# Two transposes moved behind the fourth attention product, with residuals ahead of normalizations and the fifth weight block behind the first left half

## The chip, the cores and the metric

The kernel runs on one core of one Trainium2 chip. The metric is the device time of one execution in microseconds; before the change it is 353.28 us, the median of three runs (352.8 to 354.54).

## What is computed

The reference is one transformer-like layer on 2048 rows of 1024 numbers, with post-normalization. Cut to what matters:

```python
attn = jnp.einsum('ds,td->st', w1, w2) * sparse_mask        # 1024 x 1024, a band
x = layernorm(x + gelu(x @ attn + b2))                      # "attention"
w_l = dequant_kbit(qweight, lut4, 4)                        # 4-bit codes, 16 entries for each row
w_h = dequant_kbit(qweight, lut8, 8)
y = where(norm(x) > 64, x @ w_h.T, x @ w_l.T) + bias        # "ffn"
out = layernorm(x + y)
```

With these inputs no row has a norm over 64, so the kernel computes the 4-bit path alone, counts the rows (and the mask's entries outside the band) that would need more, and runs a general path behind a branch that is not taken here.

## The kernel before

**Tiles.** The 2048 rows are 16 row tiles x0 to x15 of 128 x 1024 in float32. The weight of the second product is dequantized in eight blocks of 128 output rows (numbered 0 to 7), each transposed into its 128 columns of `wT`. The identity matrix is added to the diagonal of each block (L349), so that the product contains the residual already.

**The first stage** forms `attn` on TensorE (PE) in eight band products (L464), each masked on VectorE (DVE, L486). Between them runs the dequantization of the first blocks.

**A block of the weight** is made by a generator, `dequantize_pair` (L309), which yields after each half of a block; `steps(n)` issues n halves. One half consists of three ScalarE (ACT) activations (L329, tiles `e`), one GpSimd (POOL) instruction (L333, tile `root`) and three predicated copies on DVE (L336, L337, L338). A second half ends with one more copy that selects between the two roots (L346) and the small addition of the identity (L349). `transpose_pending(left)` (L358) transposes finished blocks into `wT`: for each block eight PE transposes (L281) into two PSUM tiles `pt` and two ACT copies out of them (L282). There are four `pt` buffers in all.

**The list `todo`** (L831) gives the order of the second stage: attention 0 to 3; then left 0, attention 4, left 1, attention 5, left 2, attention 6, left 3, attention 7; then attention 8 to 11; then right 0, attention 12, and so on. The second product of row tiles 4 to 15 is done in pairs by `ffn_pair`, which the change does not touch.

- **attention n** (L577): ten PE products onto a PSUM tile `mm` that already holds `b2` (L556; `mm` has two buffers, and ACT fills them in L505, `fill_b2`); Gelu on ACT into `z` (L581; two buffers); the residual x + z on DVE with a row sum (L585); then `stats` (L383): the mean on POOL (`nm`, L387), the sum of squares on ACT (`junk`, L390), the reciprocal root on POOL (`r`, L392 and L393). The normalization on DVE (L397) and two small POOL instructions (L591, L592) are put off into a list `later`, which `now()` empties.
- **left n and right n** (`ffn_half`, L637): eight PE products of 512 columns (L599) into `mm`, and the addition of the bias on DVE (L611, `combine`). A left half reads `wT`'s blocks 0 to 3, a right half blocks 4 to 7.
- **prepare** (L858) transposes the next entry's input. For left n it transposes the normalized row tile with its columns in another order (`early{n}`); for attention n the raw one. It does so ahead of the current entry, except for left 0: `soon` is false there, and the transposes come behind attention 3.

**What sets the order.** A scheduler orders each engine's instructions by the order in the program, dependencies and estimated times, and moves them where it sees room; from attention 8 on DVE is in program order (`manual_schedule`, L871). `tc.issue_after(ins)` adds an edge that keeps the block's instructions on `ins`'s engine behind `ins`; it costs no wait. Each engine then runs its own queue strictly in order, and waits on semaphores for the others. What matters here is therefore which instruction stands ahead of which in a queue.

The lines around the change: L868 empties `pending` (blocks 2 and 3 of the weight) at attention 3, that is before its products; L582 and L889 empty `later`; L837 lists after which entries one more half block is issued:

```python
unpack_after = [("attention", n) for n in range(3)]
unpack_after += [("left", 0), ("attention", 4), ("left", 1)]
unpack_after += [("attention", 5), ("left", 2), ("attention", 6), ("left", 3)]
```

The first two of these ten halves finish block 3; blocks 4 to 7 are the other eight.

Of the kernel before, what the change touches and what calls it, by code (L numbers as in the profile page):

```python
# [32 lines left out]
EARLY = 4  # L33
# [3 lines left out]
def window(s):  # L37

    return max(0, s * P - BAND), min(D, (s + 1) * P + BAND)
# [153 lines left out]
def kernel(  # L193
# [13 lines left out]
    nc = tc.nc  # L207
# [7 lines left out]
    with ExitStack() as main:  # L215
# [60 lines left out]
        def transpose_blocks(dst, block):  # L276

            for g in range(NH):
                pt = ps_tr.tile([P, HALF // P, P], FP, tag="tr", name="pt")
                for j in range(HALF // P):  # L280
                    nc.tensor.transpose(pt[:, j, :], block(g * (HALF // P) + j), ident)  # L281
                done = nc.scalar.copy(dst[:, g * (HALF // P) : (g + 1) * (HALF // P), :], pt)  # L282
            return done

        def transpose_columns(dst, src):
            return transpose_blocks(dst, lambda k: src[:, ts(k, P)])
# [71 lines left out]
        def transpose_pending(left):  # L358

            while len(pending) > left:  # L360
                ot, w_nat = pending.pop(0)
                transpose_columns(wT[:, :, ts(ot, P)], w_nat)
# [15 lines left out]
        def steps(n):  # L378
            for _ in range(n):
                next(low, None)  # L380


        def stats(u, total):  # L383


            nm = work.tile([P, 1], FP, tag="nm", name="nm", bufs=4)
            nc.gpsimd.tensor_scalar(nm, total, -1.0 / D, None, ALU.mult)  # L387
            junk = work.tile([P, D], BF, tag="junk", name="junk", bufs=1)
            ss = work.tile([P, 1], FP, tag="ss", name="ss", bufs=4)
            nc.scalar.activation(junk, u, AF.Square, scale=float(-D), bias=total, accum_out=ss)  # L390
            r = work.tile([P, 1], FP, tag="r", name="r", bufs=4)
            nc.gpsimd.tensor_scalar(r, ss, 1.0 / D**3, EPS, ALU.mult, ALU.add)  # L392
            nc.gpsimd.tensor_tensor(r, r, minus_half, ALU.pow)  # L393
            return nm, r, ss

        def normalize(dst, u, nm, r):
            nc.vector.tensor_scalar(dst, u, nm, r, ALU.add, ALU.mult)  # L397
# [3 lines left out]
        def load_x(pool, n):  # L401
            t = pool.tile([P, D], FP, tag=f"x{n}", name=f"x{n}")
            nc.sync.dma_start(out=t, in_=x[ts(n, P), :])
            x_tiles.append(t)
# [7 lines left out]
        with tc.tile_pool(name="prod", bufs=1) as prod:  # L412
# [47 lines left out]
            for s in range(KT):  # L460
                lo, hi = window(s)
                ps = ps_mm.tile([P, D], FP, tag="mm", name="mm")
                for k in range(KT):
                    part = nc.tensor.matmul(  # L464
                        out=ps[:, : hi - lo],
                        lhsT=w1_sb[s][:, k, :],
                        rhs=w2T[:, k, lo:hi],
                        start=(k == 0),
                        stop=(k == KT - 1),
                    )  # L470
# [3 lines left out]
                if s >= KT - 2:  # L474
# [11 lines left out]
                masked = nc.vector.tensor_tensor(  # L486
                    attn[:, s, : hi - lo], ps[:, : hi - lo], masks[s][:, : hi - lo], ALU.mult
                )
                if s >= KT - 2 - AHEAD and len(first_xT) < AHEAD:

                    n = len(first_xT)
                    xT = work.tile([P, D], FP, tag="z", name="xT", bufs=2)
# [10 lines left out]
        def fill_b2():  # L503
            ps = ps_mm.tile([P, D], FP, tag="mm", name="mm")
            nc.scalar.copy(ps, b2_bc)  # L505
            with_b2.append(ps)
# [6 lines left out]
            load_x(late, n)  # L513
        nc.sync.dma_start(out=bias_bc, in_=bias.partition_broadcast(P))

        def transposed(n, tag, bufs, by_bit):
            xT = late.tile([P, KT, P], FP, tag=tag, name="xT", bufs=bufs)
            if by_bit:
                cols = x_tiles[n].rearrange("t (b s) -> t s b", s=8)
                transpose_blocks(xT, lambda k: cols[:, k, :])  # L520
            else:
                transpose_columns(xT, x_tiles[n])
            return xT
# [17 lines left out]
        def check_outside(s):  # L541

            for raw, _, _, _, i in outside_band(s):
                nc.scalar.activation(raw, raw, AF.Abs, accum_out=outside[:, i : i + 1])

        def band_rows(xT):

            if not with_b2:
                fill_b2()
            ps = with_b2.pop(0)  # L550
            for s in range(KT):
                lo, hi = window(s)
                for h in range(NH):
                    a, b = max(lo, h * HALF), min(hi, (h + 1) * HALF)
                    if a < b:
                        nc.tensor.matmul(  # L556
                            out=ps[:, a:b],
                            lhsT=xT[:, s, :],
                            rhs=attn[:, s, a - lo : b - lo],
                            start=False,  # L560
                            stop=hi == D or (h == 0 and window(s + 1)[0] >= HALF),
                            skip_group_check=True,
                        )
            return ps
# [5 lines left out]
        def now():  # L570
            while later:
                later.pop(0)()
# [4 lines left out]
        def attention(n, xT, meanwhile=nothing):  # L577
            xt = x_tiles[n]
            ps = band_rows(xT)
            z = work.tile([P, D], FP, tag="z", name="z", bufs=2)  # L580
            nc.scalar.activation(z, ps, AF.Gelu)  # L581
            now()  # L582
            meanwhile()
            total = work.tile([P, 1], FP, tag="total", name="total", bufs=4)
            nc.vector.scalar_tensor_tensor(xt, z, 1.0, xt, ALU.mult, ALU.add, accum_out=total)  # L585
            nm, r, ss = stats(xt, total)

            def rest():
                normalize(xt, xt, nm, r)

                nc.gpsimd.tensor_tensor(ssq[:, n : n + 1], r, r, ALU.mult)  # L591
                nc.gpsimd.tensor_tensor(ssq[:, n : n + 1], ssq[:, n : n + 1], ss, ALU.mult)  # L592

            later.append(rest)
# [42 lines left out]
        def ffn_half(n, xT, h):  # L637
            ps = ps_mm.tile([P, D], FP, tag="mm", name="mm")
            product(ps[:, :HALF], xT, h)
            now()  # L640
            combine(n, h, ps[:, :HALF], bias_bc[:, ts(h, HALF)])
            if h == 1:
                finish_rows(n)
# [187 lines left out]
        todo = [("attention", n) for n in range(4)]  # L831
# [2 lines left out]
        todo += [("attention", n) for n in range(4 + EARLY, SOON)]  # L834
        for m in range(EARLY):
            todo += [("right", m), ("attention", SOON + m)]
        unpack_after = [("attention", n) for n in range(3)]  # L837
        unpack_after += [("left", 0), ("attention", 4), ("left", 1)]
        unpack_after += [("attention", 5), ("left", 2), ("attention", 6), ("left", 3)]

        kept = {}
        rows, blocks = {}, {}
# [15 lines left out]
        def prepare(what, n):  # L858
            if what == "attention":
                return first_xT[n] if n < AHEAD else transposed(n, "xT", 2, False)  # L860
            if what == "left":
                kept[n] = transposed(n, f"early{n}", 1, True)
            return kept[n]

        ready = prepare(*todo[0])
        ordered = main.enter_context(ExitStack())
        for i, (what, n) in enumerate(todo):
            if (what, n) == ("attention", EARLY - 1):  # L868
                transpose_pending(0)
            if (what, n) == ("attention", 2 * EARLY):  # L870
                ordered.enter_context(tc.manual_schedule(engines={mybir.EngineType.DVE}))  # L871
            if (what, n) == ("attention", SOON - 2):
                steps(100)
                transpose_pending(0)
                first_sb.close()
                last = main.enter_context(tc.tile_pool(name="last", bufs=1, side="right"))
                for m in range(SOON, NT):
                    load_x(last, m)
            xT = ready

            soon = i + 1 < len(todo) and todo[i + 1] != ("left", 0)
            if soon:
                ready = prepare(*todo[i + 1])
            if what == "attention":
                if n >= SOON + 1:
                    attention(n, xT, lambda: prepare_pair(EARLY, n - SOON - 1))
                else:
                    attention(n, xT)
                if n < 2 * EARLY:  # L889
                    now()  # L890
            else:
                ffn_half(n, xT, 0 if what == "left" else 1)
                if what == "right":
                    weight_sum(last, n + 1)
                    now()
            if i + 1 < len(todo) and not soon:
                ready = prepare(*todo[i + 1])
            if (what, n) in unpack_after:
                with tc.issue_after(masked.ins):
                    steps(1)  # L900
        first_ps.close()
        ps_pair = main.enter_context(
# [54 lines left out]
```

## Time and profile before

| | before |
|---|---|
| median of 3 runs | 353.28 us |
| the profiled execution | 353.46 us |
| its span in the profile | 351.7 us |
| PE busy | 325.6 us (93%) |
| DVE busy | 210.3 us (60%) |
| ACT busy | 179.1 us (51%) |
| POOL busy | 116.1 us (33%) |
| mean granted TensorE clock | 0.99 |

The span is what the profile covers; 1.8 us of the execution lie around it. A row of the profile's timeline gives a start, a duration, the engine, the line, the output and inputs, a count, and in brackets the idle time before it with what ended it. Rows of PE products overlap a little, since matmuls are pipelined; two passes are counted for each float32 product, so an attention product has twenty. The duration of DVE and ACT rows contains their write-out, and the next instruction can start about 0.1 us before the end of a row. "PEclk" is the share of the full TensorE clock that was granted.

### The profile page before, as it was taken

Reading aid. Unit: us, or ns where it says so; the run is one execution under the profiler, and the core shown is the slowest. Engines: PE = TensorE matmul, PEld = TensorE weight load, DVE = VectorE, ACT = ScalarE, POOL = GpSimd, SP = SyncE. Lnnn points to the kernel's source line nnn. Section 1 sums busy time; section 2 is a strip of 40 time slices with the busy share of each in tenths; the row PEclk is TensorE's granted clock in tenths of the full one; section 3 lists DMA queues with packets and bytes.
Section 4 is the critical chain, followed back from the end, with each engine's and each line's share of the span. In section 5 each row is a group of like instructions: output and inputs, shape, how many; then the busy total and the mean of one; then the engine's idle time right before and its main releaser. Section 6 shows DMA issues by size and latency. Waiting matters only on the chain.

```text
span 351.7 us, 3697 instructions
## 1 busy us (share of the span) xinstructions
PE 325.6 (93%) x1227; PEld 201.7 (57%) x1228; DVE 210.3 (60%) x310; ACT 179.1 (51%) x257; POOL 116.1 (33%) x162
## 2 busy tenths in 40 slices
PE   6699979759999999999999989999999998999990
PEld 6587769655775679856665534444444444444460
DVE  0659898878999853435667763544535615632342
ACT  4796987879989959856435401214115024033020
POOL 1812432793264443234352711403104005014010
PEclk9999999989999999999999999999999999999997
DMA  8999209400000000603056334253553441431103
GB/s 253 320 316 383 109 25 376 197 2 0 0 3 0 0 2 0 239 3 108 37 188 210 118 110 129 91 209 108 211 171 123 185 160 59 177 123 60 60 16 116
DMA packets 28475, 43.91 MB, mean 125 GB/s; under 512 B 7584, under 2 KB 20640, under 8 KB 28448
## 3 DMA queue, kind: packets, MB, share of 16 engines
q1 hardware_dynamic: 26832, 42.66, 35.3%
q10 hardware_dynamic: 1616, 0.93, 0.9%
q8 instruction: 12, 0.20, 0.2%
q14 instruction: 15, 0.12, 0.1%
HBM read 28.90 MB, written 14.68 MB: 124 GB/s over the span
## 4 chain that ended last, share of the span: by engine, by line
PE 72%; DVE 10%; DMA 7%; POOL 5%; issue 3%; ACT 1%; SPq 0%; POOLq 0%; DVEq 0%
PE u L716 21%; PE mm L599 16%; PE mm L556 13%; PE w L716 10%; PE v L716 6%; PE pt L281 6%; DMA w_raw<-in_L_attn_w_dram 2%; DMA w_sb<-in_L_attn_w_dram 2%; DVE e L336 2%; POOL root L333 2%; DMA x<-in_L_attn_x_dram 2%; PE mm L464 1%; DVE squares L666 1%; DVE root L346 1%; DVE root L338 1%
## 5 line engine op out<-in xcount | busy, mean ns | idle before, releaser
L390 ACT ACTIVATE junk<-x,total 128x1024 bf16<-128x1024 f32 x31 | 35.6, 1150 | 60.8 <-DVE total L624 26.8
L556 PE MATMUL mm<-attn,xT 128*128 128x198 f32 (+2 forms) x320 | 61.2, 347 | 1.1 <-ACT mm L505 1.1
L329 ACT ACTIVATE e<-v,lt,diff 128x1024 f32<-128x1024 uint8 x48 | 56.9, 1244 | 4.7 <-issue 3.2
L556 PEld LDWEIGHTS mm<-attn,xT 128*128 128x128 f32 x320 | 53.5, 193 | 8.4 <-issue 1.9
L599 PE MATMUL mm<-wT,xT 128*128 128x512 f32 x128 | 56.3, 592 | 0.0
L333 POOL TENSOR_SCALAR root<-v,diff,lt 128x1024 f32<-128x1024 uint8 x16 | 37.0, 2320 | 31.9 <-DVE v L299 21.1
L387 POOL TENSOR_SCALAR nm<-total 128x1 f32<-128x1 f32 x31 | 19.8, 637 | 82.8 <-DVE x L585 54.2
L716 PE MATMUL u<-t,halves 128*128 128x512 f32 x96 | 43.3, 593 | 1.0 <-DVE x L736 1.0
L599 PEld LDWEIGHTS mm<-wT,xT 128*128 128x128 f32 x128 | 23.8, 190 | 26.8 <-issue 26.1
L702 POOL TENSOR_TENSOR halves<-halves 128x512 f32<-128x512 f32 x6 | 9.5, 1586 | 84.0 <-DVE halves L699 49.8
L698 ACT COPY halves<-rows 128x1024 f32<-128x1024 f32 x6 | 6.3, 1042 | 54.8 <-DMA rows<-there 54.8
L716 PEld LDWEIGHTS u<-t,halves 128*128 128x128 f32 x96 | 18.2, 190 | 24.3 <-issue 22.2
L464 PE MATMUL mm<-w2T,w_sb 128*128 128x268 f32 (+1 forms) x128 | 29.2, 377 | 2.6 <-ACT w2T L282 1.2
L666 DVE STREAM_TRANSPOSE squares<-x 128x1024 f32<-128x1024 f32 x12 | 24.3, 2027 | 10.8 <-DMA there<-squares 10.8
L397 DVE TENSOR_SCALAR x<-x,nm,r 128x1024 f32<-128x1024 f32 x16 | 13.0, 814 | 29.1 <-POOL r L393 24.5
L464 PEld LDWEIGHTS mm<-w2T,w_sb 128*128 128x128 f32 x128 | 22.8, 189 | 6.5 <-ACT w2T L282 2.6
L281 PE MATMUL pt<-ident,x 128*128 128x128 f32 x160 | 22.0, 283 | 3.8 <-ACT wT L282 3.8
L336 DVE COPY_PREDICATED e<-v,e 128x1024 f32<-128x1024 uint8 x16 | 23.6, 1475 | 1.6 <-ACT e L329 1.6
L585 DVE SCALAR_TENSOR_TENSOR x<-z,x 128x1024 f32<-128x1024 f32 x16 | 20.5, 1281 | 6.6 <-ACT z L581 6.6
L337 DVE COPY_PREDICATED root<-v,e 128x1024 f32<-128x1024 uint8 x16 | 21.0, 1315 | 3.6 <-POOL root L333 3.6
L281 PEld LDWEIGHTS pt<-ident,x 128*128 128x128 f32 x160 | 19.5, 155 | 5.9 <-ACT wT L282 4.2
L338 DVE COPY_PREDICATED root<-v,e 128x1024 f32<-128x1024 uint8 x16 | 22.8, 1427 | 0.2
(93 smaller groups left out, 441.2 us busy)
## 6 DMA issues: line engine op xcount, KB each, us to landing
x<-in_L_attn_x_dram SPq DMA_DIRECT2D x16, 512.0 KB, 7.5
out_dram<-o SPq DMA_DIRECT2D x14, 512.0 KB, 2.6
there<-squares SPq DMA_DIRECT2D x12, 512.0 KB, 3.1
rows<-there SPq DMA_DIRECT2D x48, 128.0 KB, 2.9
w_raw<-in_L_attn_w_dram SPq DMA_DIRECT2D x8, 512.0 KB, 7.0
w_sb<-in_L_attn_w_dram SPq DMA_DIRECT2D x3, 1024.0 KB, 7.8
w_sb<-in_L_attn_w_dram SPq DMA_DIRECT2D x2, 512.0 KB, 7.0
x<-_L_attn_sparse_mask_dram SPq DMA_DIRECT2D x2, 413.0 KB, 3.7
```

The source lines that it names most:

```text
L281: nc.tensor.transpose(pt[:, j, :], block(g * (HALF // P) + j), ident)
L329: nc.scalar.activation(entry[j], plane(0), AF.Identity, scale=d_k, bias=l_k)
L333: nc.gpsimd.tensor_scalar(entry[j], plane(0), d_k, l_k, ALU.mult, ALU.add)
L336: nc.vector.copy_predicated(entry[2], plane(1), entry[3])
L337: nc.vector.copy_predicated(root, plane(1), entry[1])
L338: nc.vector.copy_predicated(root, plane(2), entry[2])
L390: nc.scalar.activation(junk, u, AF.Square, scale=float(-D), bias=total, accum_out=ss)
L464: part = nc.tensor.matmul(out=ps[:, : hi - lo], lhsT=w1_sb[s][:, k, :], rhs=w2T[:, k, lo:hi], start=(k == 0), stop=(k == KT - 1),)
L556: nc.tensor.matmul(out=ps[:, a:b], lhsT=xT[:, s, :], rhs=attn[:, s, a - lo : b - lo], start=False, stop=hi == D or (h == 0 and window(s + ...
L599: nc.tensor.matmul(out=ps, lhsT=xT[:, k, :], rhs=wT[:, k, ts(h, HALF)], start=(k == 0), stop=(k == KT - 1),)
L666: nc.vector.transpose(out=t, in_=x_tiles[n].rearrange("t (c j k) -> t c k j", c=Q, k=KT))
L716: nc.tensor.matmul(out=ps, lhsT=a[:, k, :], rhs=b[:, k, :], start=start and k == 0, stop=stop and k == KH - 1, skip_group_check=True,)
```

## The change

It moves instructions and removes none: the counts on every engine stay as they are.

1. The transposes of weight blocks 2 and 3 (`transpose_pending(0)`) go from the front of attention 3 to behind its last product, together with the transposes of x0 for left 0 (`prepare`), all behind `issue_after(behind_mm[0].ins)`.
2. For attention 0 to 8 `now()` is called behind the residual and `stats`, not ahead of them; the separate `now()` after attention 0 to 7 goes. So the normalization of a row tile is issued behind the next tile's residual, or behind the current one's statistics, as the scheduler finds room.
3. Block 4 of the weight begins behind left 0 instead of attention 2, behind the second ACT copy of x0's transposes (`behind_copy[0]`); all later halves move on by one place, and the last one follows attention 7.

```diff
+        behind_copy = [None]
+
         def transposed(n, tag, bufs, by_bit):
             ...
-                transpose_blocks(xT, lambda k: cols[:, k, :])
+                behind_copy[0] = transpose_blocks(xT, lambda k: cols[:, k, :])
...
+        behind_mm = [part]
+
         def band_rows(xT):
             ...
-                        nc.tensor.matmul(
+                        behind_mm[0] = nc.tensor.matmul(
...
             nc.scalar.activation(z, ps, AF.Gelu)
-            now()
+            if n > 2 * EARLY:
+                now()
             meanwhile()
             ...
             nm, r, ss = stats(xt, total)
+
+            if n <= 2 * EARLY:
+                now()
...
-        unpack_after = [("attention", n) for n in range(3)]
-        unpack_after += [("left", 0), ("attention", 4), ("left", 1)]
-        unpack_after += [("attention", 5), ("left", 2), ("attention", 6), ("left", 3)]
+        unpack_after = [("attention", 0), ("attention", 1), ("left", 0), ("attention", 4)]
+        unpack_after += [("left", 1), ("attention", 5), ("left", 2), ("attention", 6)]
+        unpack_after += [("left", 3), ("attention", 7)]
...
-            if (what, n) == ("attention", EARLY - 1):
-                transpose_pending(0)
...
-                if n < 2 * EARLY:
-                    now()
...
             if i + 1 < len(todo) and not soon:
-                ready = prepare(*todo[i + 1])
+                with tc.issue_after(behind_mm[0].ins):
+                    transpose_pending(0)
+                    ready = prepare(*todo[i + 1])
             if (what, n) in unpack_after:
-                with tc.issue_after(masked.ins):
+
+                first = behind_copy[0] if (what, n) == ("left", 0) else masked
+                with tc.issue_after(first.ins):
                     steps(1)
```

In the built programs the order on PE is, before: attention 2, blocks 2 and 3, x0, x4, attention 3, left 0, x1, attention 4; and after: attention 2, attention 3, blocks 2 and 3, x0, x4, left 0, x1, attention 4. Behind that, the transposes of block 4 move from behind left 2 to behind attention 6, and those of block 5 from behind left 3 to behind attention 7; the rest of PE's order is the same. SP's queue of DMAs is the same throughout. On ACT, the three `e` rows of block 4's first half no longer stand among the attention rows, and from attention 5 on `fill_b2` stands behind the `junk` of the tile before in more places. On DVE the residuals of x1 to x3 move ahead of copies of blocks 3 and 4, and block 4's first six copies move from before the normalization of x3 to behind it.

## The prediction

> **What bounds the kernel now.** I read the page's slices first.
>
> ```profile
> PE   6699979759999999999999989999999998999990
> DVE  0659898878999853435667763544535615632342
> PEclk9999999989999999999999999999999999999997
> ```
>
> From the tenth slice on PE is busy throughout, so what shortens the time must shorten PE's work or start its full stretch earlier. The ninth slice, 70 to 79 us, has a dip in PE and the one dip in the granted clock. The timeline of PE shows the place.
>
> ```profile
> 61.55 3.76 PE L556 MATMUL mm<-attn,xT 128*128 128x198 f32 x20
> 65.14 1.04 PE L281 MATMUL pt<-ident,root 128*128 128x128 f32 x8
> 68.80 1.06 PE L281 MATMUL pt<-ident,root 128*128 128x128 f32 x8 [2.62 <-DVE root L349]
> 69.83 0.71 PE L281 MATMUL pt<-ident,x 128*128 128x128 f32 x4
> 74.37 2.46 PE L281 MATMUL pt<-ident,x 128*128 128x128 f32 x12 [3.83 <-ACT wT L282]
> 76.62 4.61 PE L556 MATMUL mm<-attn,xT 128*128 128x198 f32 x20
> 81.06 7.03 PE L599 MATMUL mm<-wT,xT 128*128 128x512 f32 x16
> ```
>
> Attention 2 ends at 65.14. PE then waits 2.62 us for block 3 (L349) and 3.83 us for an ACT copy, while attention 3 stands behind both. What does that cost beyond the 6.45 us? The busy time by stretches shows it (PEclk is the third number from the end).
>
> ```profile
> 72.00:74.00 2.00, 0.00 (x0) 0.00 (x0) 2.00 (x5) 1.40 (x3) 2.00 (x1) 1.00 0.00 0
> 74.00:76.00 2.00, 1.63 (x10) 1.64 (x11) 2.00 (x1) 2.00 (x4) 2.00 (x2) 0.73 0.03 8
> 76.00:78.00 2.00, 2.00 (x8) 1.89 (x7) 0.02 (x1) 2.00 (x5) 1.75 (x4) 0.50 0.00 0
> 78.00:80.00 2.00, 2.00 (x12) 1.82 (x12) 1.67 (x6) 2.00 (x3) 1.03 (x3) 0.92 0.00 0
> ```
>
> After the long gap the clock is at half. Twelve transposes take 2.46 us, where eight take 0.87 from start to start elsewhere (so 1.31 for twelve), and attention 3 takes 4.40 for the usual 3.60: 1.95 us. The second gap is ACT's, and ACT's is DVE's:
>
> ```profile
> 72.60 1.15 ACT L390 ACTIVATE junk<-x,total 128x1024 bf16<-128x1024 f32 x1 [2.82 <-DVE x L585]
> 73.75 1.54 ACT L282 COPY wT<-pt 128x512 f32<-128x512 f32 x3
> ```
>
> The copies that free `pt` stand behind `junk` of x2, which waits for the residual at 71.34, which stood behind x1's normalization at 70.61, which waited for POOL.
>
> **Early part of the change.** I lay the built order of after along the rows of before; up to x0's normalization (60.64) nothing differs. Starts, in us:
>
> Gelu of x1: block 4's `e` row (1.25 us) no longer stands ahead of it, so it starts when attention 1 ends, 60.05 instead of 60.83. Its residual now precedes L338: it follows L337 at 62.6 instead of 64.77 and ends at 63.8. `junk` of x1 takes 1.15 to 65.0, `fill_b2` for attention 3 another 0.95 to 66.0. So attention 3 runs from 66.05 to 69.65: 0.9 us of idle PE.
>
> x1's normalization now precedes block 3's L349. POOL needs two small instructions of 1.18 beside busy DVE and one of 0.57, from 63.85 to 67.0; L397 ends at 67.75 and L349 at 68.05, against 68.60 before. That is ahead of the transposes, at 69.65. Then three L299 (0.2 each) and x2's residual, 68.65 to 69.9, 2.7 us earlier than before.
>
> ACT: `junk` of x2 to 71.1, Gelu of x3 to 72.0, three copies of 0.48 to 73.45. PE's sixteen transposes of blocks 2 and 3 end at 71.4 and fill all four `pt`; x0's first four wait for the first copy until 72.6 (1.2 idle), the next two groups follow the copies to 74.0. The fourth copy stands behind `junk` of x3, whose residual waits for Gelu of x3 and x2's normalization (POOL ready at 72.15): residual 72.95 to 74.2, `junk` to 75.4, copy to 75.9. PE idles 1.95, does the last four transposes, and left 0 starts at 76.45 instead of 81.06: 4.6 us earlier. The account agrees: idle 0.9 + 1.2 + 1.95 = 4.05 against 6.45 is 2.4, and 1.95 of slow clock is 4.35. I take 4.5.
>
> Does the clock stay up? In before, the 2.62 us gap left it at 1.00 and the 3.83 us gap did not; the longest now is 1.95. The Trainium skill speaks against that in one place: "TensorE: Matmul & The Clock Gate", in "A second HAM failure mode: psum-queue depth-cycling", says that repeated short idles between groups of products, too, make the clock oscillate. By that page's window of about 3.4 us one half-clock window would cost some 1.7 us (an estimate from the page). The rows of before disagree so far: between 46 and 56 us gaps of 0.71 and 1.12 us stand close together and the clock is 1.00. By the rows the price is between 0 and the 1.95 above; I take 0.
>
> **Late part: block 4 is later.** Left halves read blocks 0 to 3 alone, so its delay is free for them. Blocks 4 to 7 need 4 x 7 copies, all now behind x3's normalization. POOL has two roots ahead of that tile's `nm`, from 73.1; they took 5.59 us together before, so L397 of x3 comes between 78 and 79.6, and block 4's first copy at about 79.3 (its `e` row on ACT, behind the transposes' copies, ends at 79.0). In before, six of the copies were already done at 86.2. From the first one DVE has, by start-to-start rows: 28 copies of 1.2 (33.6), twelve steps of 0.13 where a copy needs the one before (1.6), four L349 of 0.3, residuals of x4 to x6 (3 x 1.14), three L397 of 0.73, four `combine` of 0.6: 44.4. ACT makes an `e` every 1.14 us, six for a block, between its copies and fills: laid out in its queue from 77.8 on, the third `e` of block 4 ends at 81.3, the sixth and the third of block 6 late as well, and DVE waits three times (0.6 + 1.0 + 0.5). It also waits for `r` of x4 and x6 (1.9, since a root is ahead in POOL's queue, and 0.9): 4.9 in all. Sum 49.3; the same recipe for before, from 83.53 to L349 of block 7 at 128.30, is within 0.3 when three copies beside a POOL root are taken at 1.65. I add half of that (0.7): L349 of block 7 ends at 129.3 against 128.3 before.
>
> ```profile
> 128.00 0.39 DVE L349 TENSOR_TENSOR root<-root,ident 128x128 f32<-128x128 f32 x1
> 128.30 0.69 DVE L611 SCALAR_TENSOR_TENSOR x<-mm,bias_bc 128x512 f32<-128x512 f32 x1
> 132.17 1.23 DVE L585 SCALAR_TENSOR_TENSOR x<-z,x 128x1024 f32<-128x1024 f32 x1 [3.18 <-ACT z L581]
> ```
>
> Before, DVE idled here 3.18 us, and attention 9 started at 136.19. PE would now want it at 131.6. But x7's residual stands behind block 7 on DVE (129.3 to 130.45), `junk` of x7 behind it on ACT (to 131.6), and one transpose's copy and `fill_b2` for attention 9 behind that (0.48 + 0.95): 133.05. So PE waits 1.4 us. The queue behind it, `fill_b2` for attention 11, comes 10.0 us after attention 9 before; with Gelu and residual of x8 waiting in the same chain it comes some 0.4 later. Net: 4.5 - 1.4 - 0.4 = 2.7 us.
>
> **The rest costs nothing.** x7's normalization moves behind x8's residual, and no one reads x7 until its `squares`. The later transposes of blocks 4 and 5 (0.87 each) move inside a busy PE. SP's queue has the same order; the loads of x12 to x15 wait for the last blocks' transposes on PE (issued at 141.84) and move with PE, as do the pairs. If they did not move, attention 12 would wait at its transposes (149.96) for up to the 2.7 gained.
>
> The profiled execution of before took 353.46 (span 351.7 and 1.76 around it), 0.18 over the median. 353.46 - 2.7 = 350.76, or 350.6 beside the median of 353.28.
>
> **Rivals.**
>
> The late wait is not there: if DVE's copies run 1.4 to 1.8 us ahead of my sum, all of 4.5 stays: 348.8. For it: DVE idled 3.18 us at that place. Against: 28 copies instead of 22 are left when the half begins.
>
> The late wait eats the gain: with the 49.3 us longer by 2.7, the time is 353.3. Eight more copies at 1.65 instead of 1.31 us would give that.
>
> Slower: POOL's four roots fall beside DVE's copies throughout. L338 beside a root took 2.17 and 2.15 us against 1.31; two copies for each of four roots at +0.85 are 6.8, 6.1 more than I counted, and the fills of attention 6 to 9 wait in turn: 350.6 + 6.1 = 356.7. It decides from 4.5 us of extra copy time on. Against: four roots fell in the same stretch of before, at 1.65 at worst.
>
> The gap does not close: transposes still wait for ACT long enough for the half clock. Then 1.95 is paid again, partly in the shadow of the late wait: 351.3 to 352.5.
>
> **How the numbers follow.** The main case has 0.56 (349.8 to 351.4), no late wait 0.13, gain eaten 0.17, slower 0.08, gap stays 0.06. About 0.5% (1.8 us, so 351.5) is what a measurement of this kernel can tell from no change. Faster: 0.56 + 0.13 + 0.03 = 0.72; same: the eaten gain and half of the last, 0.20; slower 0.08. The range, 348.7 to 352.9, leaves out the slower case and the ends of two others.
>
> **What would show it.** Right: attention 3 directly behind attention 2 with about 0.9 us between, left 0 near 76.5, a granted clock of 1.00 throughout 60 to 90 us, a wait of PE for `mm` (ACT, L505) of about 1.4 us ahead of attention 9 near 133. Wrong: a clock below 1 there, PE waiting for `fill_b2` already at attention 5 to 7, or left 0 later than 79.

## The result, and the profile after

The changed kernel takes 358.27 us (median of four runs, 355.92 to 358.48) against 353.23 us for the kernel before on the same chip: a ratio of 1.0117, with an interval of 1.0087 to 1.0148 (the two medians alone give 1.0143). The prediction was 350.6 us and faster. One of the four runs lies 2.3 us below the other three, and the runs of several kernels below spread as widely, so a difference of two medians can be off by some 2 us. The experiments ran on other chips, where the kernel before took 353.45, 353.31 and 353.95 us in the first, second and third part of the experiments. The profiled execution took 358.36 us, its span is 356.6 us against 351.7. The slices of its page:

```profile
PE   6799989959999987999999998999999999999990
DVE  0579898846888885336476853554635525733342
PEclk9999999969999998999999999999999999999997
```

The dip in the ninth slice is still there, and there is a new, shallower one in the sixteenth (134 to 143 us), in PE and in the clock. The timeline of PE shows both places:

```profile
65.94 3.86 PE L560 MATMUL mm<-attn,xT 128*128 128x198 f32 x20 [0.72 <-ACT mm L505]
69.64 1.91 PE L281 MATMUL pt<-ident,root 128*128 128x128 f32 x16
74.39 2.51 PE L281 MATMUL pt<-ident,x 128*128 128x128 f32 x12 [2.84 <-ACT wT L282]
77.67 1.11 PE L281 MATMUL pt<-ident,x 128*128 128x128 f32 x4 [0.77 <-ACT wT L282]
78.58 8.59 PE L607 MATMUL mm<-wT,xT 128*128 128x512 f32 x16
...
132.40 3.86 PE L560 MATMUL mm<-attn,xT 128*128 128x198 f32 x20 [1.24 <-ACT mm L505]
136.10 1.04 PE L281 MATMUL pt<-ident,x 128*128 128x128 f32 x8
139.56 5.54 PE L560 MATMUL mm<-attn,xT 128*128 128x198 f32 x20 [2.43 <-ACT mm L505]
```

Attention 3 indeed runs at 65.94, ahead of the transposes. But these then wait 2.84 us for ACT's copies, left half 0 begins at 78.58 (before: 81.06) and takes 8.59 us where all others take 7.03. So x1's transposes begin at 87.00, only 0.93 us earlier than before. Then PE waits for `fill_b2` (L505) 1.24 us ahead of attention 8 and 2.43 us ahead of attention 9, and attention 9 takes 5.54 us instead of 3.76. The first product of the pairs begins at 200.24 us, 4.93 later than before's 195.31, and that goes through to the end. The early part gained 0.93, the late part lost 5.86.

The granted clock (third number from the end) in stretches of 2 us:

```profile
74.00:76.00 2.00, 1.61 (x9) 1.61 (x10) 1.87 (x3) 1.40 (x4) 1.92 (x3) 0.72 0.00 0
76.00:78.00 2.00, 1.23 (x7) 0.83 (x6) 0.00 (x0) 2.00 (x5) 2.00 (x2) 0.50 0.00 0
78.00:80.00 2.00, 2.00 (x6) 1.25 (x5) 0.60 (x1) 2.00 (x5) 1.59 (x6) 0.50 0.00 0
80.00:82.00 2.00, 2.00 (x4) 0.82 (x3) 1.47 (x2) 2.00 (x3) 0.26 (x1) 0.57 0.00 0
...
138.00:140.00 2.00, 0.44 (x2) 0.44 (x3) 0.00 (x0) 2.00 (x5) 1.15 (x4) 0.93 0.00 0
140.00:142.00 2.00, 2.00 (x6) 1.61 (x5) 1.51 (x3) 2.00 (x4) 0.18 (x1) 0.50 0.00 0
142.00:144.00 2.00, 2.00 (x11) 1.92 (x10) 0.45 (x1) 1.51 (x3) 0.86 (x3) 0.71 0.00 0
```

The clock is at half behind both gaps. Counting a slice between 0.50 and 1.00 in part, it was at half for 6.8 us in the early stage and for 3.4 us at attention 9. Why does `fill_b2` come late? The timeline of ACT says what stands ahead of it in the queue:

```profile
131.33 1.02 ACT L505 COPY mm<-b_bc 128x1024 f32<-128x1024 f32 x1 [1.45 <-DVE x L619]
...
136.88 1.15 ACT L390 ACTIVATE junk<-x,total 128x1024 bf16<-128x1024 f32 x1 [2.13 <-DVE x L590]
137.93 0.19 ACT L390 ACTIVATION_READ_ACCUMULATOR junk<-x,total 128x1 f32 x1
138.03 0.56 ACT L282 COPY xT<-pt 128x512 f32<-128x512 f32 x1
138.49 1.02 ACT L505 COPY mm<-b_bc 128x1024 f32<-128x1024 f32 x1
```

Both wait for DVE: the first for a `combine` (L619, the buffer of left half 3), the second behind `junk` of x7, whose residual (L590) stands behind block 7. So the last link is DVE's chain of blocks 4 to 7. Some of its rows that begin after a wait, and its last one:

```profile
80.74 1.32 DVE L337 COPY_PREDICATED root<-v,e 128x1024 f32<-128x1024 uint8 x1 [0.53 <-ACT e L329]
...
87.20 0.69 DVE L619 SCALAR_TENSOR_TENSOR x<-mm,bias_bc 128x512 f32<-128x512 f32 x1 [1.55 <-PE mm L607]
...
99.38 0.81 DVE L397 TENSOR_SCALAR x<-x,nm,r 128x1024 f32<-128x1024 f32 x1 [1.96 <-POOL r L393]
...
128.66 0.81 DVE L397 TENSOR_SCALAR x<-x,nm,r 128x1024 f32<-128x1024 f32 x1 [1.01 <-POOL r L393]
...
135.25 0.40 DVE L349 TENSOR_TENSOR root<-root,ident 128x128 f32<-128x128 f32 x1
```

L349 of block 7 starts at 135.25 (before: 128.00). Between 80.74 and there DVE stands still 0.93 and 0.76 us for `e`, 1.55 for a `combine`, 0.93 for a root, and three times for `r` (1.96, 1.01, 1.01).

### The profile page after: what moved, and what is told of

The parts are those of the page before. It is cut to its first block, busy times and chain, and to the rows that moved or that the text cites. A ratio compares the mean times of both kernels' runs of the same rounds, so it can differ in the third digit from the quotient of the medians.

```text
span 356.6 us, 3693 instructions
## 1 busy us (share of the span) xinstructions
PE 329.1 (92%) x1227; PEld 203.3 (57%) x1228; DVE 211.2 (59%) x310; ACT 178.7 (50%) x257; POOL 114.7 (32%) x162
## 4 chain that ended last, share of the span: by engine, by line
PE 60%; DVE 17%; POOL 9%; ACT 5%; issue 4%; DMA 3%; POOLq 0%; DVEq 0%; ACTq 0%
PE u L724 20%; PE mm L607 10%; PE w L724 10%; PE mm L560 8%; PE v L724 6%; POOL root L333 4%; DVE e L336 4%; PE pt L281 3%; DVE root L338 3%; DVE root L346 2%; DMA w_raw<-in_L_attn_w_dram 2%; DVE root L337 2%; POOL nm L387 2%; DVE x L590 2%; PE mm L464 1%
## 5 line engine op out<-in xcount | busy, mean ns | idle before, releaser
L560 PE MATMUL mm<-attn,xT 128*128 128x198 f32 (+2 forms) x320 | 62.2, 351 | 5.5 <-ACT mm L505 5.5
L607 PE MATMUL mm<-wT,xT 128*128 128x512 f32 x128 | 57.8, 605 | 0.0
L333 POOL TENSOR_SCALAR root<-v,diff,lt 128x1024 f32<-128x1024 uint8 x16 | 39.5, 2476 | 44.4 <-DVE root L346 23.2
L590 DVE SCALAR_TENSOR_TENSOR x<-z,x 128x1024 f32<-128x1024 f32 x16 | 20.5, 1281 | 7.7 <-ACT z L585 7.7
L336 DVE COPY_PREDICATED e<-v,e 128x1024 f32<-128x1024 uint8 x16 | 22.7, 1422 | 3.3 <-ACT e L329 3.3
L337 DVE COPY_PREDICATED root<-v,e 128x1024 f32<-128x1024 uint8 x16 | 21.0, 1315 | 3.9 <-POOL root L333 3.4
L724 PE MATMUL v<-wT,halves 128*128 128x512 f32 x48 | 22.7, 594 | 0.0
```

The lines of the kernel that those rows point to most:

```text
L333: nc.gpsimd.tensor_scalar(entry[j], plane(0), d_k, l_k, ALU.mult, ALU.add)
L336: nc.vector.copy_predicated(entry[2], plane(1), entry[3])
L337: nc.vector.copy_predicated(root, plane(1), entry[1])
L560: behind_mm[0] = nc.tensor.matmul(out=ps[:, a:b], lhsT=xT[:, s, :], rhs=attn[:, s, a - lo : b - lo], start=False, stop=hi == D or (h == 0 ...
L607: nc.tensor.matmul(out=ps, lhsT=xT[:, k, :], rhs=wT[:, k, ts(h, HALF)], start=(k == 0), stop=(k == KT - 1),)
L724: nc.tensor.matmul(out=ps, lhsT=a[:, k, :], rhs=b[:, k, :], start=start and k == 0, stop=stop and k == KH - 1, skip_group_check=True,)
```

## The experiments

### One part at a time

Theory A: the later fifth block (part 3) is the loss, the other parts gain. Theory B: the moved transposes (part 1) are. Four kernels, each the changed one with parts put back. Parts 1 and 2, without part 3:

```diff
-        unpack_after = [("attention", 0), ("attention", 1), ("left", 0), ("attention", 4)]
+        unpack_after = [("attention", n) for n in range(3)]
...
-                first = behind_copy[0] if (what, n) == ("left", 0) else masked
+                first = masked
```

> Transposes behind attention 3 and residuals ahead of normalizations, but block 4's dequantization where before has it (behind attention 2). Theory A (the later fifth block is the loss: DVE's chain reaches block 7 some 6 us late and PE waits for fill_b2 at attentions 8 and 9): L349 of block 7 back near 128 to 130, no idle of more than 0.5 us ahead of attention 8 and at most 1.5 ahead of attention 9, the early gain of 1 to 4 us kept: 349 to 352. Theory B (the moved transposes, with POOL's roots beside DVE's copies, are the loss): PE's idle ahead of attentions 8 and 9 is still over 2 us together: 356 to 359.

Part 3 alone (`transpose_pending(0)` and the calls of `now()` where before has them):

> Block 4's dequantization behind left half 0 and each later half one place later, all else as before (transposes ahead of attention 3, normalizations first). Theory A: block 4's first copy near 80, L349 of block 7 4 to 7 us later than before's 128.3, PE idle ahead of attentions 8 and 9: 355 to 359. Theory B: DVE has room, 352.5 to 354.5.

Part 1 alone (as the first of these, and `now()` where before has it):

> Only the transposes (weight blocks 2 and 3, x0) behind attention 3. Theory A: PE does 3.6 us of attention in the stretch where it waited, left half 0 begins 1 to 3 us earlier than 81.06, late stage as before: 350 to 352.5. Theory B: as the parts 1 and 2 together, 356 to 359. If the residuals' order is what shortens the gap, this one is 1 us or more slower than parts 1 and 2 together.

Part 2 alone:

```diff
+            if (what, n) == ("attention", EARLY - 1):
+                transpose_pending(0)
...
-                with tc.issue_after(behind_mm[0].ins):
-                    transpose_pending(0)
-                    ready = prepare(*todo[i + 1])
+                ready = prepare(*todo[i + 1])
```

and block 4 where before has it.

> Only the order on DVE: residual of attentions 1 to 8 ahead of the normalization of the tile before. Both theories: within 0.7 us of before, 352.6 to 354; more if block 3's L349, now behind no normalization, lets the transposes ahead of attention 3 start earlier (down to 351.5).

| parts | median, us | ratio to before |
|---|---|---|
| 1 and 2 | 361.11 | 1.0217 (1.0191 to 1.0243) |
| 3 | 356.56 | 1.0095 (1.0068 to 1.0123) |
| 1 | 360.90 | 1.0201 (1.0153 to 1.0250) |
| 2 | 353.51 | 1.0004 (0.9991 to 1.0017) |

Both theories fall: part 1 costs 7.5 us by itself and part 3 costs 3.1, while part 2 costs nothing. The two losses sit in different places. Timeline of PE, parts 1 and 2:

```profile
70.33 5.47 PE L560 MATMUL mm<-attn,xT 128*128 128x198 f32 x20 [4.95 <-ACT mm L505]
75.64 1.91 PE L281 MATMUL pt<-ident,root 128*128 128x128 f32 x16
79.87 3.31 PE L281 MATMUL pt<-ident,x 128*128 128x128 f32 x16 [2.33 <-ACT wT L282]
86.41 8.83 PE L607 MATMUL mm<-wT,xT 128*128 128x512 f32 x16 [3.23 <-ACT xT L282]
```

All of its loss is early: x1's transposes begin 7.14 us late (95.07 against 87.93), the pairs 7.15 late, and there is no wait at attentions 8 and 9. ACT's timeline of the same kernel says why:

```profile
69.27 1.01 ACT L505 COPY mm<-b_bc 128x1024 f32<-128x1024 f32 x1
...
73.82 4.62 ACT L329 ACTIVATE e<-v,lt,diff 128x1024 f32<-128x1024 uint8 x4
78.35 1.00 ACT L585 ACTIVATE z<-mm 128x1024 f32<-128x1024 f32 x1
79.25 2.02 ACT L282 COPY wT<-pt 128x512 f32<-128x512 f32 x4
```

Four `e` rows of block 4 stand ahead of Gelu of x3 and of the copies that free `pt`. With part 3 they are gone from here; part 1 needs part 3. Part 3 alone, PE's timeline:

```profile
68.67 1.13 PE L281 MATMUL pt<-ident,root 128*128 128x128 f32 x8 [3.14 <-DVE root L349]
69.60 5.42 PE L560 MATMUL mm<-attn,xT 128*128 128x198 f32 x20
74.85 1.93 PE L281 MATMUL pt<-ident,x 128*128 128x128 f32 x16
76.68 7.13 PE L603 MATMUL mm<-wT,xT 128*128 128x512 f32 x16
...
137.25 5.54 PE L560 MATMUL mm<-attn,xT 128*128 128x198 f32 x20 [2.42 <-ACT mm L505]
```

This was the surprise. With block 4 out of the way the scheduler itself puts attention 3 ahead of x0's transposes, and left half 0 begins at 76.68, 4.38 us earlier than before: the gain that the prediction had expected from all three parts together. (0.65 us of it were there already at attention 2, which began at 60.90 in this execution and at 61.55 in before's.) The gap for block 3's L349 stays, but the transposes of block 2 are copied out while PE waits, so x0's never wait for `pt`. In exchange the late loss is there in full: 0.26, 0.80, 0.94 and 2.42 us of waits from left half 3 to attention 9, and half the clock in attention 9. Of the 4.3 us gained up to x1's transposes (83.65) the pairs, at 197.92, have lost 6.9.

Hence theory A': two separate losses. Part 3 makes DVE's chain late, which costs 5 to 7 us at attentions 8 and 9; part 1 then costs 2 to 3 us in the early stage.

### DVE's standing time, part 1, and the clock

The changed kernel without part 1:

```diff
+            if (what, n) == ("attention", EARLY - 1):
+                transpose_pending(0)
...
-                with tc.issue_after(behind_mm[0].ins):
-                    transpose_pending(0)
-                    ready = prepare(*todo[i + 1])
+                ready = prepare(*todo[i + 1])
```

> The change without its first part: transposes of the weight blocks ahead of attention 3 as in before, the other two parts kept. Theory A' (two separate losses: the later fifth block makes DVE's chain late and costs 5 to 6 us of PE wait and slow clock at attentions 8 and 9; the moved transposes cost a further 2 to 3 in the early stage, since sixteen of them and x0's then wait for ACT's copies together): as part 3 alone, 355.5 to 357.5, left half 0 near 76.7, PE waiting over 4 us in all ahead of attentions 7 to 9. Rival (the late wait comes from the residuals' order together with the later block): 353 to 354.5.

Measured: 355.69 us, 1.0073 (1.0056 to 1.0089). Left half 0 begins at 76.49, PE waits 0.80, 0.93 and 2.42 us ahead of attentions 7, 8 and 9. Together with part 3 the residuals' order does not matter for the late wait, and part 1 costs 358.27 - 355.69 = 2.6 us between the medians, but only 0.4 between the lowest runs (355.92 and 355.49).

Next, no work is removed from the changed kernel; only the normalizations of x3 to x6 are moved in DVE's queue, behind the `combine` that follows, so that `r` is there when DVE comes to them:

```diff
             product(ps[:, :HALF], xT, h)
-            now()
-            combine(n, h, ps[:, :HALF], bias_bc[:, ts(h, HALF)])
+            if h == 1:
+                now()
+            added = combine(n, h, ps[:, :HALF], bias_bc[:, ts(h, HALF)])
             if h == 1:
                 finish_rows(n)
+            else:
+                with tc.issue_after(added.ins):
+                    now()
```

> The changed kernel, with the normalization of x3 to x6 put behind the combine of the left half that follows, so that DVE does not stand waiting for r from POOL. Theory A': the waits of DVE for r (1.96, 1.01, 1.01 and 0.93 in the changed kernel) go, L349 of block 7 ends at 130 to 132 instead of 135.65, PE's idle ahead of attentions 8 and 9 falls from 3.7 to under 1 us and attention 9 takes 3.8 instead of 5.5: 352.5 to 354.5. Rival B' (not DVE's chain but the fill's place in ACT's queue, or the clock alone, makes the loss): within 1 us of the changed kernel, 357.3 to 359.3.

> Parts 2 and 3 without part 1, and the normalization of x3 to x6 behind the next combine. Theory A': the early gain of 4.4 us (left half 0 near 76.7) stays, and DVE's chain loses 5 to 7 us of waits for r, part of them given back as waits for e from ACT: L349 of block 7 at 127.5 to 130.5, PE's idle ahead of attentions 8 and 9 under 1.5 us: 348.8 to 352. Rival B': as parts 2 and 3, 355.5 to 357.5.

Measured: 353.08 us (1.0003, 0.9988 to 1.0018) with all three parts, 352.32 us (0.9989, 0.9967 to 1.0011) without part 1. The second misses its expected range by 0.3 us: left half 0 begins at 77.32, L349 of block 7 at 130.67, and PE still waits 1.81 us ahead of attention 9. In the first, DVE's timeline has no wait for `r` from block 4's first copy on, nor the one for the `combine`, and its last row of block 7 is

```profile
130.94 0.39 DVE L349 TENSOR_TENSOR root<-root,ident 128x128 f32<-128x128 f32 x1
```

4.3 us earlier than in the changed kernel, from the same first copy (80.79 against 80.74). PE waits 1.69 us ahead of attention 9 and not at all ahead of attention 8, and attention 9 takes 3.86 us.

Not all of the 4.3 us is the order. In this execution left half 0 took 7.08 us instead of 8.59, so its `combine` was ready in time. The next kernel below has the changed kernel's order up to attention 8 and, in its profile, a left half 0 of 7.12 us. There too the `combine` (its L621) comes without a wait, while the waits for `r` stay (2.23, 1.01 and 1.01 us):

```profile
85.49 0.66 DVE L621 SCALAR_TENSOR_TENSOR x<-mm,bias_bc 128x512 f32<-128x512 f32 x1
...
133.81 0.39 DVE L351 TENSOR_TENSOR root<-root,ident 128x128 f32<-128x128 f32 x1
```

From its first copy (80.65) to the end of block 7 the chain takes 53.5 us, against 54.8 in the changed kernel and 50.5 in the deferred one. So the order is worth 3.0 us on DVE, and the slow left half 0 is the other 1.3. In the times the order is worth 358.27 - 353.08 = 5.2 us between the medians, 3.3 between the lowest runs and 3.9 between the highest. By each of them the kernel is back at before's time, with no work removed: the net loss of the change goes with DVE's standing time, not with DVE's work.

And the clock: sixteen more transposes of x10's last group into the same tile fill the gap ahead of attention 9.

```diff
+                for j in range(again if g == NH - 1 else 0):
+                    nc.tensor.transpose(pt[:, j % 4, :], block(g * (HALF // P) + j % 4), ident)
...
-                transpose_columns(xT, x_tiles[n])
+                transpose_columns(xT, x_tiles[n], 16 if n == 2 * EARLY + 2 else 0)
```

> The changed kernel with 16 more transposes of x10's last group into the same tile (some 1.7 us of PE work with the same result) in the gap ahead of attention 9. Theory A': the wait for fill_b2 stays where it is, only the slow clock behind it goes: attention 9 starts at 139.5 and takes 3.8 instead of 5.54, 356 to 357. Theory C (the gate is most of the loss): 355 or less. Theory D (the gap is no matter of the gate): no change, 358.3.

Measured: 356.42 us (1.0097, 1.0066 to 1.0128; four runs at 355.28, 355.52, 357.33 and 357.35).

```profile
135.53 1.91 PE L283 MATMUL pt<-ident,x 128*128 128x128 f32 x16
138.12 3.86 PE L562 MATMUL mm<-attn,xT 128*128 128x198 f32 x20 [0.68 <-ACT mm L507]
```

Attention 9 is back at 3.86 us. The clock behind this gap is some 1.7 us of the loss on PE; in the times it is 1.9 between the medians, 0.6 between the lowest runs and 1.1 between the highest. It adds to the late wait, it is not most of it. In this profile left half 0, unchanged up to there, takes 7.12 us and not 8.59, and the clock is at half for 3.4 us there and not for 6.8. That executions some 2 us apart differ by the length of this stretch fits, but was not tested.

### The fill's place, and a faster version

If the chain is block 7, x7's residual, `junk` of x7, then the fill, it can also be cut behind DVE. In the changed kernel only the statistics of x7 are issued behind attention 9's fill:

```diff
             ps = band_rows(xT)
+            if n == 2 * EARLY + 1:
+                held.pop()()
...
-            nm, r, ss = stats(xt, total)
...
+            def finish():
+                nm, r, ss = stats(xt, total)
+                def rest():
+                    ...
+                later.append(rest)
+
+            if n == 2 * EARLY - 1:
+                held.append(finish)
+            else:
+                finish()
```

> The changed kernel with only the statistics of x7 (nm, junk, r) issued behind attention 9's fill_b2, so that this fill no longer stands behind junk of x7 in ACT's queue. Theory A' with this place named (block 7, then x7's residual, then junk x7, then the fill): the wait of 2.43 us ahead of attention 9 and its slow 1.8 us go, the 1.24 us ahead of attention 8 stay: 353.3 to 355.3. Rival (the fill comes late for another reason, or attention 11's fill takes the wait over): 356.5 or more.

Measured: 354.81 us (1.0026, 1.0008 to 1.0043). That is 0.9 us above before on the same chip, where the changed kernel was 5.0 above; between the lowest runs (353.57 and 355.92) it is 2.4 less. On PE attention 9 now follows attention 8, while the wait ahead of attention 8, which has the other cause, is as it was:

```profile
132.84 3.86 PE L560 MATMUL mm<-attn,xT 128*128 128x198 f32 x20 [1.23 <-ACT mm L505]
136.54 1.04 PE L281 MATMUL pt<-ident,x 128*128 128x128 f32 x8
137.41 3.76 PE L560 MATMUL mm<-attn,xT 128*128 128x198 f32 x20
```

DVE's chain is as late as ever (L349 of block 7 at 135.69), so it is this queue place through which it reached PE. A part moves on: attention 11 waits 1.20 us for its fill.

With this and the deferred normalizations, once without part 1 and once with it, and the former also with 24 more transposes of block 2's last group in the gap ahead of block 3's:

> Parts 2 and 3, the deferred normalizations, and attention 9's fill ahead of junk x7. Theory A': the wait of 1.81 us ahead of attention 9 goes, half or more of it stays gained up to the pairs: 349.8 to 351.5. Rival: the wait moves to attention 11 (its fill now stands behind two junks): 352 to 353.

> The changed kernel with all three parts, the deferred normalizations and the early fill: with the late wait out of the way it shows what part 1 itself is worth. Theory A' (part 1 costs 1 to 2.5 us in the early stage): 0.7 to 2 us slower than the same without part 1, 351 to 352.8. If part 1 is worth what the prediction gave it: equal or faster.

> The one before with 24 more transposes of block 2's last group into the same tile (some 2.6 us of PE work with the same result), in the gap ahead of block 3's transposes. If that gap's slow clock is what attention 3 and the transposes around it lose (5.14 us where 3.76 is usual, and 0.4 more in block 3's transposes), it gains 1.2 to 2: 348.2 to 350. If the extra work delays the copies of ACT, or DVE's chain is the bound again: no gain, 350 to 351.5.

| kernel | median, us | ratio to before |
|---|---|---|
| parts 2 and 3, deferred, fill first | 351.01 | 0.9914 (0.9895 to 0.9933) |
| parts 1, 2 and 3, deferred, fill first | 352.18 | 0.9951 (0.9934 to 0.9968) |
| parts 2 and 3, deferred, fill first, gap filled | 349.74 | 0.9887 (0.9869 to 0.9905) |

With the late wait nearly gone, part 1 still costs 352.18 - 351.01 = 1.2 us, and here the runs of the two kernels do not overlap (350.18 to 351.48, and 351.87 to 352.65). The last one is faster than both kernels of this case, 1.1% below before. PE's timeline of it:

```profile
65.35 2.78 PE L283 MATMUL pt<-ident,root 128*128 128x128 f32 x24
68.68 1.06 PE L281 MATMUL pt<-ident,root 128*128 128x128 f32 x8 [0.55 <-DVE root L351]
69.58 3.76 PE L562 MATMUL mm<-attn,xT 128*128 128x198 f32 x20
73.18 1.93 PE L281 MATMUL pt<-ident,x 128*128 128x128 f32 x16
75.31 7.13 PE L618 MATMUL mm<-wT,xT 128*128 128x512 f32 x16 [0.20 <-ACT xT L284]
```

Transposes that compute nothing new stand where PE waited 3.17 us in the same kernel without them; attention 3 takes 3.76 us instead of 4.66, and left half 0 begins at 75.31 instead of 77.33. (0.67 us of that were there already at attention 2, at 60.88 and 61.55 in the two executions.)

## Why the prediction was wrong

**Attention 3 moves up.** Right: 65.94 with 0.72 idle, for 66.05 with 0.9.

**x2's residual at 68.65.** It came at 70.46, because POOL was not free at 63.85 as the step assumed. The root at 61.40 took 4.41 us, where the row of before had 2.23, and `nm` of x1 stood behind it; the three L299 took 1.53 us beside the next root, not 0.6. The term was taken from before, where the root took 2.23 us and the copy beside it (L338) 2.17 instead of 1.31.

**The idle times and the clock at 1.00.** Idle was 2.84 + 0.77 = 3.61 for the predicted 1.2 + 1.95 = 3.15; that is a small miss. The price of 0 for the clock was the larger one. The sixteen transposes of x0 and x4 lost 1.0 + 0.5 us (2.51 us for the first twelve, where eight take 1.04 and sixteen 1.91 at the full clock, so 1.48 for twelve; 0.91 to the next row for 0.44), and left half 0 lost 1.56. With the idle this makes 3.5, and the 4.5 became 0.93. The prediction had inferred from the 2.62 us gap of before that shorter gaps are free, and laid the warning aside; the gap that it put at 1.2 us was then 2.84. (Its upper price of 1.95 is a little high, too: it sets a duration, 2.46, against a time from start to start, 1.31. Start to start the loss in before is 0.9 + 0.8.) The warning was the Trainium skill's page "TensorE: Matmul & The Clock Gate", section "A second HAM failure mode: psum-queue depth-cycling", by which repeated short idles make the clock oscillate. Here gaps of 2.84 and 0.77 us, and of 1.24 and 2.43 us, stood close together and the clock was at half behind them, but no run shows that it was the repetition. The estimate of some 1.7 us for one half-clock window, worked out from that page, agrees with the 1.78 us that attention 9 lost in 3.4 us at half clock; the early stage was at half for twice as long and lost 1.0 + 0.5 + 1.56.

**Where the early gain comes from.** The prediction laid out the three parts together and never asked what each gives, nor did a rival. Part 3 alone begins left half 0 at 76.68, and part 1 costs in every company that was run (7.5, 2.6 and 1.2 us between the medians). Its sixteen transposes and those of x0 and x4 stack up on four `pt` buffers, whose copies stand behind `junk` of x2. The prediction had seen that queue and counted it, but compared only with before, not with part 3 without part 1.

**The late chain: first copy at 79.3, then 50.0 us.** The failing step, together with the price of 0 for the clock. The first copy came at 80.74, since its `e` on ACT, which the sum had ended by 79.0, began at 79.43 behind the copies of the transposes. From there to the end of L349 of block 7 (129.3 predicted, about 135.55 measured) it took 54.8 us. Waits for `r` were 4.0 us instead of 2.8; the 1.55 us for left 0's `combine`, itself late through the slow clock, and 0.93 for a root were not in the sum; the copies beside roots cost 1.5 (2.04 and 2.09 for 1.31) instead of 0.7; waits for `e` were 1.7 instead of 2.1. These are 4.1 of the 4.8 us; the rest is in small pieces. The deferred normalizations confirm it: without the waits for `r` and for the `combine` the chain is 50.5 us long. That this is nearly the 50.0 of the sum is partly luck, since the sum holds 2.8 us of waits for `r`, and this chain has none but three copies of 2.03 to 2.13 us.

**PE's wait ahead of attention 9.** The mechanism was right (block 7, x7's residual, `junk`, fill) and is shown by the kernel that cuts it. Its size was 2.43 for 1.4, with 1.78 of slow clock behind it. Attention 8's wait was not foreseen: its fill needs the buffer of left half 3, whose `combine` stands on DVE behind x6's normalization and a copy of block 7.

**The slower rival** came closest (fills wait in turn, 356.7 us) and had the cause wrong: four roots were to slow eight copies by 6.8 us, and they slowed two, by 1.5. What it should have priced was DVE standing behind POOL's and PE's results.

## What to carry to other kernels

When work on an in-order engine is put off to free an early stage, add up how long the engine stands idle there and what it has to catch up: a late chain with 3 us to spare turns each lost microsecond beyond that into a wait of the engine that sets the time. Before giving such a change up, look at which rows of that chain begin after a wait; moving those rows back in the queue gave 3 to 5 us here without removing any work. Measure each part of a combined change alone and in company: the part named first here cost time in both.

## What the runs showed of the hardware

**The clock and the length of a gap.** Behind gaps of 2.62 us (before) and 2.65 us (part 2 alone), both ahead of block 3's transposes, the rows ran at full speed. Behind 2.42 and 2.43 us ahead of attention 9, with shorter gaps 7 us earlier, and behind 2.84 us ahead of x0's transposes, they ran at half. And the same gap ahead of x0's transposes left the clock at half for 6.8 us in the changed kernel (2.84 us), for 3.4 us in the deferred one (2.84 us), and not at all in the deferred one with the fill first (2.87 us):

```profile
74.42 1.64 PE L281 MATMUL pt<-ident,x 128*128 128x128 f32 x12 [2.87 <-ACT wT L282]
```

So the length of a gap alone does not decide in this range; what does was not isolated. By slices of 1 us between 60 and 160 us, each stretch at half clock in the profiles of this case lasts 3.4 us or twice that. Transposes put into the gap kept the clock up in both places (attention 9 took 3.86 us instead of 5.54, attention 3 took 3.76 instead of 4.66).

**A root on POOL beside copies on DVE.** The same instruction on 128x1024 at the same place took 2.23 us while DVE's copy beside it took 2.17 instead of 1.31 (before), and 4.41 us while the copies L337 and L338 beside it stayed at 1.31 and L346 took 1.99 (the changed kernel). In the first case the two copies followed each other, in the second the residual stood between them; no run separated the cause.
